# Softmax row sums of a two-layer graph attention: from matmuls against ones to transfers over the partitions

## The chip, the cores and the metric

The kernel runs on one core of one Trainium2 chip. The metric is the device time of one launch in microseconds. Engines are named as in the profile: PE is TensorE (PEld its weight loads), DVE is VectorE, ACT is ScalarE, POOL is GpSimd, SP is SyncE. SP and POOL also issue the transfers (DMA); POOL issues those that add to what stands at the destination.

## What is computed

32 graphs of 512 nodes with 256 features each go through two layers of masked attention with 8 heads of 32 features. Layer 0 masks with the symmetrised adjacency and the diagonal, and has a feed-forward block behind it; layer 1 masks with the adjacency alone. Each layer ends in a residual and a layer norm. All arithmetic is in 32-bit floats.

```python
x = _layernorm(x + L0(x, adj))
x = _layernorm(x + L1(x, adj))
# L0: q, k, v = x @ Wqkv.T + bqkv, heads of 32
#     attn = softmax(where(allowed, q @ k.T / sqrt(32), -inf)); ctx = attn @ v
#     x = LN(x + ctx @ Wo.T + bo); x = LN(x + relu(x @ W1.T + b1) @ W2.T + b2)
# L1: the same attention with mask adj != 0, out = ctx @ Wo.T + bo
```

The part that matters here is the softmax's denominator, the row sum of `exp(scores)` over the 512 keys, for each of 512 queries, 8 heads, 2 layers and 32 graphs.

## The kernel before

Attention is computed transposed. For a group `hg` of four heads (`HPC` = 4) and a block `kc` of 128 keys (`NQ` = 4), one *beat* `k = hg * 4 + kc` makes a tile `p[k]` of 128 keys by 4 heads by 512 queries: `scores` (L345, then the exponential on ACT, L349), `masked` (L354, DVE multiplies by the mask), `product` (L362, TensorE adds values times `p` into PSUM; at the last block ACT copies the result to `cT`, L372). So a layer has 8 beats, and the row sums run over the partitions (keys)[...].

The row sums are made in two steps. First, the four tiles of a group are added into one: `pair` (L377) is a transfer that POOL issues and that adds `p[k + 1]` onto `p[k]`, 1 MB; `fold` (L381) is an addition on DVE. `pair(0)`, `pair(2)` and `fold(2, 2, 0)` leave the sum of group 0 in `p[2]`; `fold(3, 6, 7)`, `pair(4)` and `fold(3, 3, 4)` leave that of group 1 in `p[3]`. Then `sums` (L402) multiplies the tile by a matrix of ones on TensorE, head `j` into the 32 rows from `32 * j` of a PSUM tile, so that every one of these rows holds the sums of that head.

`divide(hg)` (L414 to L421) then runs on DVE: a transpose in blocks of 32 turns the sums of 512 queries into 16 columns, a reciprocal is taken of these, a second transpose spreads it over the rows, and `cT` is multiplied by it. POOL adds the sums and reciprocals to `total` (L417, L418), a running check at the end of the program that tells whether a slower general version is needed. `project` (L461) multiplies `cT` by the output weights; `out0` and `out1` (L449 and the statistics L430, L431) add the residual and start the layer norm. `root` (L436, L437) is the layer norm's inverse square root, on POOL; `norm1` to `norm4` and `offset` (L527) use it. `mlp` (L502) is the second half of the feed-forward block, `out2` its residual.

For the very last attention (`final()`: graph 31, layer 1) `pair` and `fold` do nothing, and `sums` goes over all four tiles with matmuls.

The order is written out by hand: every engine works through its instructions in program order, and each waits for the semaphores of what it needs. `period(a, b, c, d, e)` is one such list, with five graphs in it at different stages: `a` is finishing layer 1, `b` does the feed-forward of layer 0 and starts layer 1, `c` starts layer 0, `d` is loaded and sorted (`load`, `flip`, `sort`, `join`, `entries`, `masks`), `e` is cast. It is called 29 times; `opening` and `closing` hold the first two and last two graphs. SP has its own queue of loads in the same program order and works as far ahead as buffers allow. The tiles `p` have 8 buffers, the PSUM tiles of tag `d`, which the sums share with most other matmuls, have 3.

Of the kernel before, what the change touches and what calls it, by code (L numbers as in the profile page):

```python
# [9 lines left out]
F32 = mybir.dt.float32  # L10
# [4 lines left out]
ALU = mybir.AluOpType  # L15
AX = mybir.AxisListType
# [11 lines left out]
def kernel(ctx: ExitStack, tc: tile.TileContext, t: dict, out: bass.AP):  # L28
# [36 lines left out]
    total = const.tile([P, N // HD], F32, name="total")  # L65
# [84 lines left out]
    def plain(pools: ExitStack):  # L150
        work = pools.enter_context(tc.tile_pool(name="work", bufs=2))
        small = pools.enter_context(tc.tile_pool(name="small", bufs=4))
# [24 lines left out]
        class Graph:  # L177
# [159 lines left out]

            def scores(self, layer, k):
                if k == 0:
                    self.layer, self.p, self.acc = layer, {}, {}  # L340
                hg, kc = divmod(k, NQ)
                s = ps_s.tile([P, HPC, N], F32, tag="s", name=f"psS_{self.b}_{k}")
                for j in range(HPC):
                    at = slice(j * HD, (j + 1) * HD)
                    nc.tensor.matmul(  # L345
                        s[:, j, :], self.kT[at, hg, kc * P : (kc + 1) * P], self.qT[at, hg, :], start=True, stop=True
                    )
                p = work.tile([P, HPC, N], F32, tag="p", name=f"p_{self.b}_{k}", bufs=8)
                nc.scalar.activation(p, s, AF.Exp, scale=SCALE)  # L349
                self.p[k] = p  # L350
# [32 lines left out]
            def add(self, dst, a):  # L383

                if not self.final():
                    nc.gpsimd.dma_start(out=self.p[dst], in_=self.p[a], accum_op=ALU.add)

            def final(self):

                return self.b == B - 1 and self.layer == 1  # L390

            def sums(self, k, hg, first=False, last=False):

                if first:
# [14 lines left out]

            def divide(self, hg):  # L410


                sT = small.tile([P, N // HD, HD], F32, tag="sT", name=f"sT_{self.b}_{hg}", bufs=1)
                nc.vector.transpose(sT.rearrange("p a b -> p (a b)"), self.total[hg])  # L414
                r = small.tile([P, N // HD], F32, tag="r", name=f"r_{self.b}_{hg}")
                nc.vector.reciprocal(r, sT[:, :, 0])
                nc.gpsimd.tensor_tensor(total, total, sT[:, :, 0], ALU.add)  # L417
                nc.gpsimd.tensor_tensor(total, total, r, ALU.add)  # L418
                rT = small.tile([P, N], F32, tag="sT", name=f"rT_{self.b}_{hg}", bufs=1)
                nc.vector.transpose(rT, r[:, :, None].to_broadcast([P, N // HD, HD]))  # L420
                nc.vector.tensor_tensor(self.cT[:, hg, :], self.cT[:, hg, :], rT, ALU.mult)  # L421
# [120 lines left out]
        def period(a, b, c, d, e):  # L542
# [33 lines left out]
            b.root(3, 3, 4)  # L576
# [125 lines left out]
            b.pair(4)  # L702
            c.norm3(1)
            c.norm3(0)
            b.divide(0)


        def opening(a, b, c, d):
# [60 lines left out]
            b.query_key(0, 0, 0)  # L769
            b.cast()  # L770
            a.fold(2, 2, 0)
            a.fold(3, 6, 7)

            b.scores(0, 0)
            a.fold(3, 3, 4)
            a.sums(2, 0, first=True, last=True)
            a.product(6)
            b.scores(0, 1)
            a.residual()
            a.product(7)  # L780
            a.sums(3, 1, first=True, last=True)
            a.divide(0)
            a.divide(1)
            b.scores(0, 2)
            b.query_key(0, 1, 1)
            a.project(0, 0)
            a.out0(0)
            a.out0(1)
# [89 lines left out]
            a.transpose(a.x2, 1)  # L878
            b.fold(3, 6, 7)
            b.fold(2, 2, 0)  # L880
            c.join(0, 0)
            a.query_key(1, 0, 0, 0)
            a.query_key(1, 0, 0, 1)
# [5 lines left out]
            a.query_key(1, 1, 1)  # L889
            a.scores(1, 1)  # L890
            b.fold(3, 3, 4)
            c.join(0, 1)
# [3 lines left out]
            b.divide(0)  # L896
            b.divide(1)
            a.product(0)
            a.scores(1, 2)
            c.value(0, 1)  # L900
# [3 lines left out]
            a.masked(1, 1)  # L904
            a.masked(1, 2)
            a.masked(1, 3)
            b.project(0, 0)
            c.query_key(0, 0, 1)
            b.project(0, 1)
# [24 lines left out]
            b.norm1(3)  # L934
            a.masked(1, 5)
            a.fold(2, 2, 0)
            a.masked(1, 4)
            b.hidden(0, 6)
            b.hidden(0, 4)
# [15 lines left out]
            b.norm2(0)  # L955
            b.norm2(1)
            b.root(3, 0, 2)
            a.divide(0)
            a.pair(4)
            b.norm3(1)  # L960
            b.norm3(0)
# [1 line left out]
        def closing(a, b, c):  # L963
# [12 lines left out]
            a.fold(3, 6, 7)  # L976
            c.masked(0, 0)
            a.fold(3, 3, 4)
            a.sums(3, 1, first=True, last=True)
            c.product(0)  # L980
            c.masked(0, 1)
# [5 lines left out]
            c.once1()  # L987
            c.masked(0, 3)
            c.pair(0)
            a.divide(1)  # L990
# [6 lines left out]
            a.project(1, 0)  # L997
            c.scores(0, 6)
            c.product(2)
            b.root(2, 2, 3)  # L1000
            c.pair(2)
            a.project(1, 1)
            a.out1(0)
# [17 lines left out]
            b.query_key(1, 0, 0, 1)  # L1021
            c.masked(0, 7)
            c.fold(2, 2, 0)
            c.masked(0, 6)
            a.offset(0, 2)
            c.fold(3, 6, 7)
            c.fold(3, 3, 4)
            b.query_key(1, 1, 1)

            b.scores(1, 0)  # L1030
# [9 lines left out]
            b.scores(1, 5)  # L1040
            a.norm4(0)
            c.sums(3, 1, first=True, last=True)
            c.divide(0)
            a.offset(2, 4)
            c.divide(1)
            b.value(1, 0)
            a.norm4(2)
            a.norm4(3)
            b.scores(1, 4)
            c.project(0, 0)  # L1050
            c.out0(0)
            b.query_key(1, 1, 0, 1)
# [68 lines left out]
            b.masked(1, 7)  # L1121
            b.pair(4)
            b.fold(2, 2, 0)
            b.fold(3, 6, 7)
            c.query_key(1, 1, 0, 0)
            c.query_key(1, 0, 0, 1)
# [6 lines left out]
            c.scores(1, 3)  # L1133
            c.value(1, 0)
            b.fold(3, 3, 4)
            b.divide(0)
            b.sums(3, 1, first=True, last=True)
            c.scores(1, 2)
            c.query_key(1, 1, 1)
            b.divide(1)  # L1140
            b.residual2()
            c.residual2()
            c.masked(1, 3)
# [3 lines left out]
            c.masked(1, 1)  # L1147
            c.value(1, 1)
            c.scores(1, 5)
            b.project(1, 0)  # L1150
            c.masked(1, 0)
            c.masked(1, 5)
# [264 lines left out]
```

## Time and profile before

| | us |
|---|---|
| median of 3 runs (lowest, highest) | 3075.76 (3073.19, 3076.84) |
| span of the profiled execution | 3072.4 |
| PE busy | 3049.0 (99%) |
| DVE busy | 2648.1 (86%) |
| ACT busy | 1707.3 (56%) |
| POOL busy | 1039.0 (34%) |
| row-sum matmuls (L402), busy, 1072 records | 139.8 |
| additions by transfer (L377), 189 of 1 MB | 7.7 each, issue to landing |
| time from one period's start to the next | 95.8 |

The page gives the span from the first to the last instruction; the profiled execution's own time is not given beside it, so the runs' median, 3.4 us above the span, stands for what lies around it. A matmul of 32-bit floats leaves two records. Busy time is the time in which an engine has an instruction running; four matmuls on separate quarters of the array overlap, so the mean of one record (598 ns for L402) is longer than the time by which it moves the next one on. DMA has a mean busy share of about 0.7 of the 16 engines in the middle of the run.

### The profile page before, as it was taken

Reading aid. Unit: us, or ns where it says so; the run is one execution under the profiler, and the core shown is the slowest. Engines: PE = TensorE matmul, PEld = TensorE weight load, DVE = VectorE, ACT = ScalarE, POOL = GpSimd, SP = SyncE. Lnnn points to the kernel's source line nnn. Section 1 sums busy time; section 2 is a strip of 40 time slices with the busy share of each in tenths; the row PEclk is TensorE's granted clock in tenths of the full one; section 3 lists DMA queues with packets and bytes.
Section 4 is the critical chain, followed back from the end, with each engine's and each line's share of the span. In section 5 each row is a group of like instructions: output and inputs, shape, how many; then the busy total and the mean of one; then the engine's idle time right before and its main releaser. Section 6 shows DMA issues by size and latency. Waiting matters only on the chain. (4 is left out here: it accounts for less than half of the span.)

```text
span 3072.4 us, 44237 instructions
## 1 busy us (share of the span) xinstructions
PE 3049.0 (99%) x17218; PEld 1728.9 (56%) x17218; DVE 2648.1 (86%) x3458; ACT 1707.3 (56%) x1983; POOL 1039.0 (34%) x1254
## 2 busy tenths in 40 slices
PE   8999999999999999999999999999999999999998
PEld 4555655556555555555555555655556555555564
DVE  6798889888889888898888988889888889888887
ACT  5455565555556555565556655565555556555554
POOL 1333333433334332343323333333433334332332
PEclk9999999999999999999999999999999999999999
DMA  9876677666767666676666766667766767666543
GB/s 207 155 141 129 116 141 145 140 123 126 136 138 148 121 131 124 138 154 122 133 124 136 148 134 131 114 141 145 139 124 126 136 137 148 120 131 124 117 83 70
DMA packets 341064, 406.54 MB, mean 132 GB/s; under 512 B 149616, under 2 KB 315632, under 8 KB 316144
## 3 DMA queue, kind: packets, MB, share of 16 engines
q0 software_dynamic: 95824, 282.09, 51.2%
q1 hardware_dynamic: 245024, 121.56, 16.1%
q8 instruction: 137, 2.24, 0.3%
q14 instruction: 79, 0.65, 0.1%
HBM read 89.01 MB, written 33.55 MB: 40 GB/s over the span
## 5 line engine op out<-in xcount | busy, mean ns | idle before, releaser
L349 ACT ACTIVATE p<-psS 128x2048 f32<-128x2048 f32 x512 | 962.2, 1879 | 657.1 <-PE psS L345 655.4
L354 DVE TENSOR_TENSOR p<-p,m 128x2048 f32<-128x2048 f32 x512 | 1155.4, 2279 | 8.4 <-ACT p L349 8.2
L436 POOL TENSOR_SCALAR rs<-mv 128x2 f32<-128x2 f32 (+1 forms) x320 | 326.3, 1020 | 940.6 <-DVE mv L431 939.7
L345 PE MATMUL psS<-qT,kT 32*128 32x512 f32 x4096 | 583.9, 640 | 2.8 <-ACT p L349 1.3
L362 PE MATMUL psA<-p,v 128*32 128x512 f32 x4096 | 492.7, 598 | 0.9 <-ACT cT L372 0.7
L502 PE MATMUL psF<-w_L_gnn_W,hT 128*128 128x256 f32 x2048 | 468.5, 382 | 0.0
L481 PE MATMUL psH<-xT,w_L_gnn_W 128*128 128x256 f32 x2048 | 467.3, 384 | 0.7 <-DMA w_L_gnn_W<-in_L_gnn_W_dram 0.7
L502 PEld LDWEIGHTS psF<-w_L_gnn_W,hT 128*128 128x128 f32 x2048 | 383.8, 190 | 123.0 <-issue 76.4
L481 PEld LDWEIGHTS psH<-xT,w_L_gnn_W 128*128 128x128 f32 x2048 | 381.4, 190 | 120.3 <-issue 47.9
L381 DVE TENSOR_TENSOR p<-p,p 128x2048 f32<-128x2048 f32 x189 | 429.5, 2286 | 6.4 <-DMA p<-p 4.7
L345 PEld LDWEIGHTS psS<-qT,kT 32*128 32x128 f32 x4096 | 159.9, 182 | 300.5 <-issue 117.2
L437 POOL TENSOR_TENSOR rs<-rs,neg_half 128x2 f32<-128x2 f32 (+1 forms) x320 | 299.6, 936 | 26.8
L362 PEld LDWEIGHTS psA<-p,v 128*32 128x32 f32 x4096 | 109.9, 109 | 315.3 <-issue 234.5
L489 ACT ACTIVATE hT<-psH,c_L_gnn_b 128x256 f32<-128x256 f32 x512 | 215.2, 472 | 120.6 <-PE psH L481 117.3
L417 POOL TENSOR_TENSOR total<-total,sT 128x16 f32<-128x16 f32 x128 | 28.4, 222 | 732.0 <-DVE sT L414 732.0
L461 PE MATMUL psO<-w_L_gnn_Wo,cT 128*128 128x256 f32 x1024 | 241.0, 383 | 0.9 <-DVE cT L421 0.9
L332 PE MATMUL psQK_None<-xT,w_L_gnn_Wqkv 128*128 128x512 f32 x512 | 238.4, 598 | 2.4 <-DMA w_L_gnn_Wqkv<-in_L_gnn_Wqkv_dram 2.4
L372 ACT COPY cT<-psA 128x512 f32<-128x512 f32 x128 | 75.0, 586 | 280.7 <-PE psA L362 280.7
L377 POOL DMA_DIRECT2D p<-p x189 | 188.2, 996 | 117.8 <-PE psA L362 108.7
L449 DVE TENSOR_TENSOR y<-psF,x 128x256 f32<-128x256 f32 x128 | 53.9, 421 | 200.1 <-PE psF L502 197.6
L461 PEld LDWEIGHTS psO<-w_L_gnn_Wo,cT 128*128 128x128 f32 x1024 | 189.3, 190 | 52.0 <-DVE cT L421 23.0
L430 DVE BATCH_NORM_STATS2 st<-y 128x6 f32<-128x256 f32 x384 | 164.3, 428 | 13.1
(68 smaller groups left out, 2930.8 us busy)
## 6 DMA issues: line engine op xcount, KB each, us to landing
p<-p POOLq DMA_DIRECT2D x189, 1024.0 KB, 7.7
x<-in_x_dram SPq DMA_DIRECT2D x64, 512.0 KB, 5.1
x<-bov POOLq DMA_DIRECT2D x64, 512.0 KB, 9.2
code<-in_adj_dram POOLq DMA_DIRECT2D x32, 512.0 KB, 6.6
m<-code SPq DMA_DIRECT2D x32, 512.0 KB, 5.6
x<-s_L_gnn_ln_b POOLq DMA_DIRECT2D x32, 512.0 KB, 10.4
x<-s_L_gnn_b POOLq DMA_DIRECT2D x32, 512.0 KB, 5.4
out_dram<-x SPq DMA_DIRECT2D x32, 512.0 KB, 9.1
```

Source lines behind the costliest of these rows:

```text
L332: nc.tensor.matmul(ps, w[:, i, c * P : (c + 1) * P], self.xT[:, i, at], start=(i == 0), stop=(i == ND - 1))
L345: nc.tensor.matmul(s[:, j, :], self.kT[at, hg, kc * P : (kc + 1) * P], self.qT[at, hg, :], start=True, stop=True)
L349: nc.scalar.activation(p, s, AF.Exp, scale=SCALE)
L354: nc.vector.tensor_tensor(p, p, m[:, k % NQ, None, :].to_broadcast([P, HPC, N]), ALU.mult)
L362: nc.tensor.matmul(self.acc[hg][j * HD : (j + 1) * HD, :], self.v[:, kc, h * HD : (h + 1) * HD], self.p[k][:, j, :], start=(kc == 0), stop ...
L381: nc.vector.tensor_tensor(self.p[dst], self.p[a], self.p[b], ALU.add)
L436: nc.gpsimd.tensor_scalar(rs, self.mv[n][:, a:b, 1:2], EPS, None, ALU.add)
L437: nc.gpsimd.tensor_tensor(rs, rs, neg_half[:, a:b, None], ALU.pow)
L461: nc.tensor.matmul(ps[:, j, :], self.cT[:, k, at], wo[layer][:, k, :], start=(k == 0), stop=(k == ND - 1))
L481: nc.tensor.matmul(ps[:, j, :], w1[:, c, at], self.xT[:, c, h * 2 * P : (h + 1) * 2 * P], start=(c == 0), stop=(c == ND - 1),)
L489: nc.scalar.activation(self.hT[h][:, f + j, :], ps[:, j, :], AF.Relu, bias=b1[:, f + j : f + j + 1])
L502: nc.tensor.matmul(ps, self.hT[h][:, f, j * P : (j + 1) * P], w2[:, f, :], start=(f == 0), stop=(f == NF - 1))
```

## The change

The matmuls against ones go, except for the final attention. In their place `tree(k, hg)` adds over the partitions by transfers: rows 64 to 127 of the tile onto rows 0 to 63 (512 KB), then rows 32 to 63 onto rows 0 to 31 (256 KB), both issued by POOL and adding at the destination. Then SP issues four plain transfers, one for each head, which put the 32 remaining rows of head `j` into rows `32 * j` to `32 * j + 31` of a tile `part` (64 KB each). `part` has one buffer. `divide` transposes `part` instead of the PSUM tile and adds the last 32 rows with a reduction on DVE before the reciprocal. The order changes with it: each `tree` stands behind the `fold` that finishes its tile, and the two `divide` calls of a layer stand next to each other just ahead of its `project`.

The diff, with the hunks of the class and of `period`; those of `opening` and `closing` insert `tree` and move `divide` in the same way.

```diff
@@ -337,7 +337,7 @@
 
             def scores(self, layer, k):
                 if k == 0:
-                    self.layer, self.p, self.acc = layer, {}, {}
+                    self.layer, self.p, self.acc, self.parts = layer, {}, {}, {}
                 hg, kc = divmod(k, NQ)
                 s = ps_s.tile([P, HPC, N], F32, tag="s", name=f"psS_{self.b}_{k}")
                 for j in range(HPC):
@@ -385,18 +385,30 @@
                 if not self.final():
                     nc.gpsimd.dma_start(out=self.p[dst], in_=self.p[a], accum_op=ALU.add)
 
+            def tree(self, k, hg):
+
+                if self.final():
+                    return
+                p = self.p[k]
+                for rows in (P // 2, P // 4):
+                    nc.gpsimd.dma_start(out=p[:rows], in_=p[rows : 2 * rows], accum_op=ALU.add)
+                self.part = small.tile([P, N], F32, tag="part", name=f"part_{self.b}_{hg}", bufs=1)
+                for j in range(HPC):
+                    nc.sync.dma_start(out=self.part[j * HD : (j + 1) * HD, :], in_=p[:HD, j, :])
+                self.parts[hg] = self.part
+
             def final(self):
 
                 return self.b == B - 1 and self.layer == 1
 
             def sums(self, k, hg, first=False, last=False):
 
+                if not self.final():
+                    return
                 if first:
                     self.total[hg] = ps_d.tile([P, N], F32, tag="d", name=f"psR_{self.b}_{hg}")
-                beats = [k]
-                if self.final():
-                    beats = range(hg * NQ, (hg + 1) * NQ) if last else []
-                    first = True
+                beats = range(hg * NQ, (hg + 1) * NQ) if last else []
+                first = True
                 for i in beats:
                     for j in range(HPC):
                         nc.tensor.matmul(
@@ -411,10 +423,16 @@
 
 
                 sT = small.tile([P, N // HD, HD], F32, tag="sT", name=f"sT_{self.b}_{hg}", bufs=1)
-                nc.vector.transpose(sT.rearrange("p a b -> p (a b)"), self.total[hg])
+                sums = small.tile([P, N // HD], F32, tag="sums", name=f"sums_{self.b}_{hg}", bufs=2)
+                if self.final():
+                    nc.vector.transpose(sT.rearrange("p a b -> p (a b)"), self.total[hg])
+                    nc.vector.tensor_copy(sums, sT[:, :, 0])
+                else:
+                    nc.vector.transpose(sT.rearrange("p a b -> p (a b)"), self.parts[hg])
+                    nc.vector.tensor_reduce(sums, sT, AX.X, ALU.add)
                 r = small.tile([P, N // HD], F32, tag="r", name=f"r_{self.b}_{hg}")
-                nc.vector.reciprocal(r, sT[:, :, 0])
-                nc.gpsimd.tensor_tensor(total, total, sT[:, :, 0], ALU.add)
+                nc.vector.reciprocal(r, sums)
+                nc.gpsimd.tensor_tensor(total, total, sums, ALU.add)
                 nc.gpsimd.tensor_tensor(total, total, r, ALU.add)
                 rT = small.tile([P, N], F32, tag="sT", name=f"rT_{self.b}_{hg}", bufs=1)
                 nc.vector.transpose(rT, r[:, :, None].to_broadcast([P, N // HD, HD]))
@@ -553,6 +571,7 @@
             b.hidden(1, 6)
             c.masked(0, 1)
             a.fold(3, 3, 4)
+            a.tree(3, 1)
             c.once()
             c.scores(0, 2)
             c.masked(0, 2)
@@ -564,13 +583,14 @@
             c.product(0)
             b.mlp(2)
             c.residual()
-            a.divide(1)
             b.root(2, 3, 4)
-            a.project(1, 0)
             c.scores(0, 4)
             b.transpose(b.x2, 0)
             b.norm2(3)
             c.masked(0, 3)
+            a.divide(0)
+            a.divide(1)
+            a.project(1, 0)
             c.pair(0)
             b.out2(2)
             b.root(3, 3, 4)
@@ -603,6 +623,7 @@
             b.query_key(1, 0, 0, 0)
             c.masked(0, 6)
             c.fold(2, 2, 0)
+            c.tree(2, 0)
             b.query_key(1, 1, 0, 1)
             a.norm4(0)
             a.norm4(1)
@@ -621,7 +642,7 @@
             b.query_key(1, 0, 1)
             d.entries()
             c.fold(3, 3, 4)
-            c.divide(0)
+            c.tree(3, 1)
             d.load()
             d.flip(0, 0)
             d.sort(0, 0)
@@ -630,7 +651,6 @@
             c.sums(3, 1, first=True, last=True)
             b.masked(1, 2)
             b.scores(1, 1)
-            c.divide(1)
             e.cast()
             b.residual2()
             b.value(1, 0)
@@ -641,6 +661,8 @@
             c.once1()
             b.masked(1, 1)
             b.scores(1, 5)
+            c.divide(0)
+            c.divide(1)
             c.project(0, 0)
             c.project(0, 1)
             b.scores(1, 3)
@@ -688,6 +710,7 @@
             c.mlp(1)
             b.product(3)
             b.fold(2, 2, 0)
+            b.tree(2, 0)
             b.masked(1, 4)
             c.out2(0)
             c.out2(1)
@@ -702,7 +725,6 @@
             b.pair(4)
             c.norm3(1)
             c.norm3(0)
-            b.divide(0)
 
 
         def opening(a, b, c, d):
...
```

More of the change, by code (lines that the diff above doesn't have):

```diff
@@ L771, in opening @@
             a.fold(2, 2, 0)
+            a.tree(2, 0)
             a.fold(3, 6, 7)
@@ L775, in opening @@
             a.fold(3, 3, 4)
+            a.tree(3, 1)
             a.sums(2, 0, first=True, last=True)
@@ L781, in opening @@
             a.sums(3, 1, first=True, last=True)
+            b.scores(0, 2)
+            b.query_key(0, 1, 1)
             a.divide(0)
             a.divide(1)
-            b.scores(0, 2)
-            b.query_key(0, 1, 1)
             a.project(0, 0)
@@ L880, in opening @@
             b.fold(2, 2, 0)
+            b.tree(2, 0)
             c.join(0, 0)
@@ L891, in opening @@
             b.fold(3, 3, 4)
+            b.tree(3, 1)
             c.join(0, 1)
@@ L895, in opening @@
             b.sums(3, 1, first=True, last=True)
-            b.divide(0)
-            b.divide(1)
             a.product(0)
@@ L906, in opening @@
             a.masked(1, 3)
+            b.divide(0)
+            b.divide(1)
             b.project(0, 0)
@@ L936, in opening @@
             a.fold(2, 2, 0)
+            a.tree(2, 0)
             a.masked(1, 4)
@@ L957, in opening @@
             b.root(3, 0, 2)
-            a.divide(0)
             a.pair(4)
@@ L978, in closing @@
             a.fold(3, 3, 4)
+            a.tree(3, 1)
             a.sums(3, 1, first=True, last=True)
@@ L989, in closing @@
             c.pair(0)
-            a.divide(1)
             c.masked(0, 4)
@@ L996, in closing @@
             b.root(2, 3, 4)
-            a.project(1, 0)
             c.scores(0, 6)
@@ L1000, in closing @@
             b.root(2, 2, 3)
+            a.divide(0)
+            a.divide(1)
+            a.project(1, 0)
             c.pair(2)
@@ L1023, in closing @@
             c.fold(2, 2, 0)
+            c.tree(2, 0)
             c.masked(0, 6)
@@ L1027, in closing @@
             c.fold(3, 3, 4)
+            c.tree(3, 1)
             b.query_key(1, 1, 1)
@@ L1042, in closing @@
             c.sums(3, 1, first=True, last=True)
-            c.divide(0)
             a.offset(2, 4)
-            c.divide(1)
             b.value(1, 0)
@@ L1049, in closing @@
             b.scores(1, 4)
+            c.divide(0)
+            c.divide(1)
             c.project(0, 0)
@@ L1123, in closing @@
             b.fold(2, 2, 0)
+            b.tree(2, 0)
             b.fold(3, 6, 7)
@@ L1135, in closing @@
             b.fold(3, 3, 4)
-            b.divide(0)
+            b.tree(3, 1)
             b.sums(3, 1, first=True, last=True)
@@ L1139, in closing @@
             c.query_key(1, 1, 1)
-            b.divide(1)
             b.residual2()
@@ L1149, in closing @@
             c.scores(1, 5)
+            b.divide(0)
+            b.divide(1)
             b.project(1, 0)
```

## The prediction

> **What bounds the kernel now.** I read the page first, then the busy time by stretch, then the timelines of one period in the middle, then the list of waits.
>
> ```profile
> PE 3049.0 (99%) x17218; PEld 1728.9 (56%) x17218; DVE 2648.1 (86%) x3458; ACT 1707.3 (56%) x1983; POOL 1039.0 (34%) x1254
> ```
>
> TensorE has no idle time: 100.00 of 100 us in nearly every stretch of the middle. One period of the hand-written order lasts 95.8 us (the same addition to `total` stands at 1701.04 and at 1796.84 on POOL), and there are 29 periods. That TensorE is full doesn't yet mean that less TensorE work shortens the period, so I look for the second limit.
>
> ```profile
> 1736.92 0.69 DVE L421 TENSOR_TENSOR cT<-cT,rT 128x512 f32<-128x512 f32 x1
> ...
> 1774.55 0.42 DVE L449 TENSOR_TENSOR y<-psF,x 128x256 f32<-128x256 f32 x1 [4.06 <-PE psF L502]
> ```
>
> ```profile
> 1737.33 3.72 PE L461 MATMUL psO<-w_L_gnn_Wo,cT 128*128 128x256 f32 x16
> ...
> 1770.90 3.62 PE L502 MATMUL psF<-w_L_gnn_W,hT 128*128 128x256 f32 x16
> 1774.44 1.06 PE L362 MATMUL psA<-p,v 128*32 128x512 f32 x8
> ```
>
> The first fence is VectorE's timeline, the second TensorE's (start, duration, operation, idle time before it and what ended it). The division of the second head group (L421) ends at 1736.92 + 0.69 = 1737.6, and the projection that needs it (L461) is what TensorE works on from 1737.33, its first half of the contraction needing the other group only. TensorE's second `mlp` (L502) ends at 1774.5, and VectorE, which waited 4.06 us for it, starts `out2(1)` at 1774.55. So there is a ring: TensorE from the projection to `mlp(1)`, 37.1 us; VectorE from `out2(1)` to the next division, 1737.6 + 95.8 - 1774.55 = 58.85 us, nearly without a gap. 37.1 + 58.85 is the period again. **Both the full TensorE and this ring bind.** The list of waits says so too:
>
> ```profile
> DVE y L449 <- PE psF L502: 197.6, 62, 4.9
> PEld psO L461 <- DVE cT L421: 23.0, 30, 1.0
> ```
>
> VectorE waits at one point of each period (two waits, 6.4 us), and the projection's weights wait for the division about once in each: 30 times.
>
> [...]
>
> **The change, part by part.**
>
> *TensorE.* 126 row sums go (64 layer passes of two groups, less the last pass). One moves the next matmul on by 0.88 to 1.00 us (L402 at 1697.29, its successor at 1698.17; the others in the same way), 0.93 on average: 3.7 us a period, 117 us in all. A PSUM buffer is freed too; nothing in the waits asks for one, so I give it nothing.
>
> *VectorE.* `divide` gets a reduction of 128x512. Nearest rows (busy us, mean ns, idle before):
>
> ```profile
> L354 DVE TENSOR_TENSOR p<-p,m 128x2048 f32<-128x2048 f32 x512 | 1155.4, 2279 | 8.4 <-ACT p L349 8.2
> ...
> L421 DVE TENSOR_TENSOR cT<-cT,rT 128x512 f32<-128x512 f32 x128 | 88.6, 692 | 8.7
> ```
>
> [...] I take 0.69, four a period: **2.8 us**, all in the ring. The division now takes 2.46 (1730.40 to 1732.86) + 0.69 = 3.15 us.
>
> *Order.* `c.divide` moves behind `masked(1,0)` and `masked(1,1)`, 2.2 us each from start to start. Two multiplications that came after the projection's release now come before it: **4.4 us** in the ring. The other moved divisions (`b.divide(0)` at the end of the period, `a.divide(1)`) stay inside VectorE's part of the ring and cost nothing themselves.
>
> *POOL and SP.* Four trees a period, each two accumulating transfers (512 and 256 KB) and four plain ones of 64 KB. I need times for them:
>
> ```profile
> p<-p POOLq DMA_DIRECT2D x189, 1024.0 KB, 7.7
> ...
> x<-s_L_gnn_b POOLq DMA_DIRECT2D x32, 512.0 KB, 5.4
> ...
> kT<-v SPq DMA_DIRECT2D x248, 64.0 KB, 3.9
> ```
>
> A lone 1 MB addition keeps the engines at share 1.0 with about 200 GB/s, so 5.2 of its shortest 7.0 us are data and 1.8 fixed. [...]That makes the halves 1.8 + 2.6 = 4.4 and 1.8 + 1.3 = 3.1 us[...]. I take 5.0 and 3.5. Four plain copies: three issues of 0.6 and a landing of 2.1 to 3.9, I take 4.2 us together. All four trees add about 5.1 us each of full DMA load, 20 us on top of 0.69 x 95.8 = 66: it fits, so load is not the matter; latency is.
>
> What stands behind the waits: POOL's small operations for the layer norms, which VectorE needs at once. After a transfer the first of them is slow:
>
> ```profile
> 1702.38 0.94 POOL L377 DMA_DIRECT2D p<-p  x1
> 1704.56 2.16 POOL L436 TENSOR_SCALAR rs<-mv 128x1 f32<-128x1 f32 x1 [1.25 <-DVE mv L431]
> 1706.80 0.58 POOL L437 TENSOR_TENSOR rs<-rs,neg_half 128x1 f32<-128x1 f32 x1
> ```
>
> Both `part` tiles of a pass share one buffer: the second group's four copies wait until `divide(0)` has read the first, and SP holds the next graph's loads behind them. Those loads ran far ahead so far (x at 1709.95, its two flips from 1710.44 to 1726.7, wanted by `join` at 1743.96). Now they start at about t = 81 of the walk below; a flip (5.8), four sorting copies (2.5) and their landing (3.9) end at 94, and `join` is wanted 6.6 us after the projection's start, at 92.6: hidden but for about 1 us, which I leave to the high end. POOL has eight issues more a period, some 6 us on an engine that is a third busy: nothing, apart from the roots. `p[2]` and `p[3]` stay taken until their copies are read; by the order of the changed kernel their buffers go to `scores(0,6)`, `scores(1,6)` and `scores(1,4)`, over 8 us later: nothing, or 2 us if a copy is that late.
>
> *The walk.* t = 0 is `mlp(1)`'s end. VectorE, by the starts of the timeline:
> - `out2(1)`, `norm2`, `norm3` to 6.9; without `b.divide(0)` the additions and two multiplications end at 15.9 with `fold(3,3,4)`. Tree: first transfer 16.0 to 21.0, second issued 21.1, then two bias additions (issues until 24.4), then `root(2,3,4)`: 2.2 + 0.6 from 24.1, done 27.0. VectorE wants it in `norm2(3)` at 19.6: **stall 7.5**.
> - `masked(0,3)` to 30.4; `divide(0)`; its transpose ends at 31.2, the second copies land at 35.4: `divide(1)` **stalls 1.9**, ends 38.5. `norm3(3)` waits for a root behind `pair(0)`: **stall 1.6**.
> - The same work as before then brings `fold(2,2,0)` to its end at 58.5. Tree: 58.6 to 63.8 (behind `pair(4)`), then `root(4,2,4)` done at 67.4; `offset` wants it at 60.7: **stall 6.8**. (Before, this place had 0.97 for a transfer, which goes.)
> - `fold(3,3,4)` to 69.8, three multiplications to 76.4, `divide(0)` to 79.5. Tree 69.9, 75.0, 78.5; copies land 82.8: `divide(1)` **stalls 3.3**, ends 86.0.
>
> Against 58.85 this is +27.2: 4.4 + 2.8 + 21.1 - 1. TensorE's 37.1 us after it has no sum in it and stays, so **the period is 123 us**; the 3.7 us saved become idle time. Over 29 periods 789 us; the ten groups in opening and closing at the same 6.8 us each, 68. The profiled execution spans 3072.4, the page gives nothing around it, and the median is 3.4 above. 3072 + 857 + 3 = 3932. Some divisions at the ends stand farther from their trees; I take **3900**.
>
> **Rivals.**
> - *The transfers hide, TensorE sets the end*: 3076 - 117 = 2959. For it: TensorE is full, and 3.7 us a period really go. Against: the ring has no slack for 7.2 us of VectorE work, whatever the transfers do. It decides if the ring has at least that much. Chance 0.02.
> - *The transfers hide, the ring grows by VectorE's work alone*: 7.2 x 31.5 = 227, 3300. It needs POOL to pass the waits; its order puts the roots behind the second transfer. Chance 0.08.
> - *DMA load becomes the bound*[...]. Chance 0.03.
> - *The transfers aren't waited for, or the edit does less than it says*: 3076. Chance 0.01.
>
> The walk: 0.86.
>
> **How the numbers follow.** Low end of the walk: 4.4 and 3.1 us, roots fast (0.3), stalls about 13, +19 a period, 3670; if half of those hide, 3500. [...] Range 3500 to 4200; it leaves out the first, second, third and fourth rivals and a twentieth of the walk. A measurement of this kernel tells about 0.2% from no change. Faster 0.02, same 0.01, slower 0.97.
>
> **What would show it.** TensorE's busy time falls by about 117 to 131 us (L402's row) while its idle time rises to some 900 us, most of it put to `psO <- DVE cT`. Waits of VectorE: `z` for `rs` near 7 us, once a period; `ms` for `rs` near 7; `sT` for the part transfers 2 to 3, twice; POOL stands about 5 us at each second transfer. Wrong if POOL issues the second transfer at once, if the roots come on time, if VectorE still waits for `psF` only as now and the period is under 103 us, or if TensorE stays full.

## The result, and the profile after

The kernel after takes 4350.68 us (median of four runs, 4334.83 to 4357.13); the kernel before took 3075.05 beside it. The ratio is 1.4142, interval 1.4125 to 1.4159. The forecast was 3900 with a range of 3500 to 4200, whose upper end rested on estimates of the author that no trace of before showed: the direction came true, the size did not.

The profiled execution spans 4355.2 us. First the page: busy time by engine, and the granted TensorE clock in 40 slices.

```profile
PE 3156.8 (72%) x16210; PEld 1806.2 (41%) x16210; DVE 2764.8 (63%) x3586; ACT 1693.5 (39%) x1983; POOL 1081.0 (25%) x1506
...
PEclk8978888888888888888988888888898888988888
```

TensorE, full before, is now busy 72% of the span. Its busy microseconds rose although the row-sum matmuls (139.8 us) are gone: the mean granted clock is 0.854 instead of 0.999, and the same matmuls last longer (the output projections 430.4 us in all, 241.0 before). Read alone, that busy time hides what happened; the waits of the kernel after tell it (total us, number, longest).

```profile
PE psO L479 <- DVE cT L439: 1143.0, 127, 19.0
...
POOL p L394 <- DMA p<-p: 638.9, 123, 9.4
...
DVE sT L431 <- DMA part<-p: 525.0, 72, 17.0
...
DVE z L463 <- POOL rs L455: 211.0, 62, 8.2
...
DVE ms L545 <- POOL rs L455: 177.5, 32, 13.0
```

TensorE stands at the output projection for the division, 1143 us in all. VectorE stands at three places: for the sums' copies, and for two roots on POOL. POOL stands 638.9 / 123 = 5.2 us at each second addition, for the first to land; no trace of before showed this wait. All of these kinds of wait were forecast. Their sizes are the matter.

The mean period comes from the starts of `masks` (L222) through the middle of each trace: before (2699.1 - 612.1) / 22 = 94.9 us, after (2630.1 - 727.6) / 14 = 135.9 us, so +41.0 where the forecast had +27.2 (its 95.8 us for a period of before was a single one). Here is where VectorE stands in the second half of one period after (start, duration, operation, idle time ahead of it and what ended it).

```profile
2177.03 0.16 DVE L545 SCALAR_TENSOR_TENSOR ms<-mv,rs 128x2 f32<-128x2 f32 x1 [5.40 <-POOL rs L455]
2186.43 0.71 DVE L431 STREAM_TRANSPOSE sT<-part 128x512 f32<-128x512 f32 x1 [0.42 <-DMA part<-p]
...
2205.47 0.71 DVE L431 STREAM_TRANSPOSE sT<-part 128x512 f32<-128x512 f32 x1 [15.84 <-DMA part<-p]
```

The last line is `divide(1)` of layer 0, the end of the walk. It waits 15.84 us, where the walk had 3.3. The queues of SP and of POOL at that time say what it waits for:

```profile
2183.13 1.27 SPq L213 DMA_DIRECT2D m<-code  x1
2184.45 12.47 SPq L218 DMA_TRANSPOSE m<-code  x4
2197.47 2.42 SPq L397 DMA_DIRECT2D part<-p  x4
```

```profile
2185.87 0.78 POOL L394 DMA_DIRECT2D p<-p  x1 [5.26 <-DMA p<-p]
2186.38 0.80 POOL L204 DMA_DIRECT2D code<-in_adj_dram  x1
2186.90 1.64 POOL L169 DMA_DIRECT2D x<-bov  x1
```

SP issues the second set of copies at 2197.47, just when it is through with four transposes of the next graph's code table (12.47 us). The second addition, issued at 2185.87 beside them, lands after 11.5 us, at about 2197.4; the same transfer at another place (2175.12) takes 4.5. So SP's queue and the late addition both hold the copies back, until about the same moment, and these lines don't tell which of them counts. And POOL puts two more 512 KB transfers, `code` and `bov`, right behind it.

### The profile page after: what moved, and what is told of

The parts are those of the page before. It is cut to its first block, busy times and chain, and to the rows that moved or that the text cites. A ratio compares the mean times of both kernels' runs of the same rounds, so it can differ in the third digit from the quotient of the medians.

```text
span 4355.2 us, 44207 instructions
## 1 busy us (share of the span) xinstructions
PE 3156.8 (72%) x16210; PEld 1806.2 (41%) x16210; DVE 2764.8 (63%) x3586; ACT 1693.5 (39%) x1983; POOL 1081.0 (25%) x1506
## 4 chain that ended last, share of the span: by engine, by line
PE 32%; DMA 24%; issue 14%; DVE 12%; SPq 9%; POOL 6%; ACT 3%; POOLq 0%; DVEq 0%; ACTq 0%
DMA p<-p 12%; PE psO L479 6%; PE psF L520 5%; PE psQK_None L332 5%; PE psS L345 5%; DMA v<-in_x_dram 4%; PE psH L499 4%; SPq L397 4%; PE psA L362 4%; DMA part<-p 4%; DVE p L354 3%; ACT p L349 2%; DMA kT<-v 2%; SPq L218 2%; POOL x L169 2%
## 5 line engine op out<-in xcount | busy, mean ns | idle before, releaser
L479 PE MATMUL psO<-w_L_gnn_Wo,cT 128*128 128x256 f32 x1024 | 430.4, 591 | 1143.0 <-DVE cT L439 1143.0
L479 PEld LDWEIGHTS psO<-w_L_gnn_Wo,cT 128*128 128x128 f32 x1024 | 295.5, 304 | 1285.4 <-DVE cT L439 1216.8
L394 POOL DMA_DIRECT2D p<-p x252 | 206.5, 824 | 1297.4 <-DMA p<-p 638.9
L431 DVE STREAM_TRANSPOSE sT<-part 128x512 f32<-128x512 f32 x126 | 89.4, 709 | 526.1 <-DMA part<-p 525.0
L454 POOL TENSOR_SCALAR rs<-mv 128x2 f32<-128x2 f32 (+1 forms) x320 | 249.0, 778 | 680.0 <-DVE mv L449 678.5
L435 POOL TENSOR_TENSOR total<-total,sums 128x16 f32<-128x16 f32 x128 | 62.4, 488 | 802.6 <-DVE sums L432 779.3
L455 POOL TENSOR_TENSOR rs<-rs,neg_half 128x2 f32<-128x2 f32 (+1 forms) x320 | 243.5, 761 | 26.7
L377 POOL DMA_DIRECT2D p<-p x189 | 189.6, 1003 | 191.7 <-PE psA L362 146.3
```

The lines of the kernel that those rows point to most:

```text
L454: nc.gpsimd.tensor_scalar(rs, self.mv[n][:, a:b, 1:2], EPS, None, ALU.add)
L455: nc.gpsimd.tensor_tensor(rs, rs, neg_half[:, a:b, None], ALU.pow)
L479: nc.tensor.matmul(ps[:, j, :], self.cT[:, k, at], wo[layer][:, k, :], start=(k == 0), stop=(k == ND - 1))
```

## The experiments

Runs are compared by their medians; each ratio is to the kernel before on the same chip. Periods are means worked out as above.

### Cutting the transfers away

x1 leaves out all transfers of the trees, x2 the copies alone, x3 the additions alone.

```diff
-  for rows in (P // 2, P // 4):                                   # x1, x3
-      nc.gpsimd.dma_start(out=p[:rows], in_=p[rows : 2 * rows], accum_op=ALU.add)
-  self.part = small.tile(...); 4 x nc.sync.dma_start(...)         # x1, x2
+  self.parts[hg] = p[:, 0, :]                                    # x1, x2
```

> The changed kernel with all transfers of the trees left out (the sums are not formed: divide transposes and reduces one head of the folded tile where it lies, and the reciprocal is taken of ones). VectorE's work, the order and TensorE's work are those of the changed kernel. Ring theory: VectorE's chain is 7.2 us longer than before with nothing waited for, minus about 1, so a period of 102 to 103 us and 3270 to 3330 us in all, part of it a slower clock after TensorE's new gaps. Rival, TensorE alone sets the end: period 92 us, 2960 us. Rival, the moved order costs more than VectorE's work because other waits open: above 3400 us.

Measured: 3433.27 us, ratio 1.1168 (1.1146 to 1.1190), period 106.2. With no transfer to wait for, the kernel is still 359 us slower than before beside it (3074.11). So it isn't TensorE's own work that sets the end. Its mean granted clock is 0.950, that of before 0.999. The time lies above the ring's forecast, where the rival of the moved order had put it. (Beside the lines shown, x1 to x3 and x8 take the reciprocal of ones.)

> The changed kernel without the four plain copies of each tree (divide transposes one head of the tile after the two additions, so the sums are wrong in three heads; the reciprocal is taken of ones). POOL's stalls stay: z for rs near 6, ms for rs near 5.4 us a period. If SP's copies and what stands around them in its queue make the long wait of the second division, both waits of sT (2.65 and 15.84 us a period) nearly vanish: at most 2 us stay, -16 to -18 us a period, 3800 to 3880 us. Rival, the additions themselves land late: the waits stay at 5 us or more, above 3950 us.

Measured: 4000.66 us, ratio 1.3014 (1.2965 to 1.3062), period 124.6: over 100 us slower than expected. The waits of `sT` nearly went, as the theory said (74.8 us over the run, 525.0 after), but that of `ms` for its root rose to 290.6 us over 31 (177.5 over 32 after): part of the gain was handed on.

> The changed kernel without the two additions of each tree (the copies move rows 0 to 31 of the folded tile, so three quarters of the keys are missing from the sums; the reciprocal is taken of ones). POOL's stalls go: z and ms wait for rs under 2 us together, -10 us a period. The copies can start right behind the fold, so the second division of layer 0 waits 2 to 5 us instead of 15.84, if the latency of the tree and SP's queue add up as I think: period 110 to 114 us, 3550 to 3680 us. Rival, SP's queue alone makes the long wait (the transposes ahead of the copies take 12 us whatever the additions do): it stays near 10 us, 3750 to 3850 us.

Measured: 3616.61 us, ratio 1.1764 (1.1741 to 1.1788), period 112.1, as expected. The additions alone cost 4001 - 3433 = 567 us, the copies alone 183, both together 4351 - 3433 = 917: 167 us more than the two apart. One place where they meet is the code table: its transposes land in 4.6 us (median) with the additions alone, in 4.5 with the copies alone and in 11.1 with both. That this is the whole of the 167 us is not shown.

### The place of the divisions, without transfers

x8 is x1 with the divisions of `period` and `a.project(1, 0)` put back where before had them.

```diff
-            a.divide(0)
-            a.divide(1)
-            a.project(1, 0)
+            a.divide(1)          # behind c.residual()
+            a.project(1, 0)      # behind b.root(2, 3, 4)
-            c.divide(0)
-            c.divide(1)
+            c.divide(0)          # behind c.fold(3, 3, 4)
+            c.divide(1)          # behind b.scores(1, 1)
+            b.divide(0)          # behind c.norm3(0)
```

> The kernel of x1_no_transfers (the trees' transfers left out, so the divisors are wrong and a constant is taken in their place), with the divisions of the repeated period and a.project(1, 0) back at the places of the kernel before. x1_no_transfers took 3433 us, 357 above before. Theory 'the place is most of it': with the 4.4 us of the two masked and the 2.3 us of half clock at the projections gone, 6.7 us a period, 3200 to 3270; what is then left above 3075 is the four reductions (2.8 us a period, 80 us) and little else. Rival 'the place is worth its VectorE work alone': 4.4 us a period, about 3305. Rival 'the matmul sums that are gone from TensorE leave gaps and a lower clock wherever the divisions stand': within 60 us of 3433.

Measured: 3164.82 us, ratio 1.0299 (1.0279 to 1.0319), period 97.1. The new place costs 3433 - 3165 = 268 us, 9.1 us a period; the two `masked` put ahead of the divisions explain 4.4 of it. From the start of `out2(1)` to the end of `divide(1)` of layer 0, VectorE takes 59.9 us in x8 (1532.11 to 1592.00) and 68.3 in x1 (1553.68 to 1622.01), 8.4 more: the two `masked`, and waits that x8 doesn't have there. VectorE's timeline of x1:

```profile
1565.89 2.29 DVE L354 TENSOR_TENSOR p<-p,m 128x2048 f32<-128x2048 f32 x1 [0.82 <-ACT p L349]
...
1575.22 0.48 DVE L458 SCALAR_TENSOR_TENSOR z<-cent,rs,x 128x256 f32<-128x256 f32 x1 [0.78 <-POOL rs L450]
...
1586.60 0.41 DVE L531 TENSOR_SCALAR x<-z,mv,rs 128x256 f32<-128x256 f32 x1 [0.88 <-POOL rs L450]
1587.72 0.42 DVE L462 TENSOR_TENSOR y<-psO,x 128x256 f32<-128x256 f32 x1 [0.71 <-PE psO L474]
```

They stand ahead of the moved divisions of layer 1 and behind them: for exponents, for two roots and for the projection of layer 1 (1.35 us in most other periods). With a second wait of 0.23 us for exponents they make 3.4 us. Why each of them is late wasn't followed up.

At layer 0 TensorE's clock has a small part in it. Here are TensorE's timelines of the projection of layer 0, first x1, then x8 in two periods in a row:

```profile
1618.97 1.22 PE L474 MATMUL psO<-w_L_gnn_Wo,cT 128*128 128x256 f32 x2 [3.85 <-DVE cT L434]
1622.07 4.88 PE L474 MATMUL psO<-w_L_gnn_Wo,cT 128*128 128x256 f32 x14 [1.88 <-DVE cT L434]
```

```profile
1494.59 4.98 PE L474 MATMUL psO<-w_L_gnn_Wo,cT 128*128 128x256 f32 x14 [2.08 <-DVE cT L434]
...
1592.05 3.29 PE L474 MATMUL psO<-w_L_gnn_Wo,cT 128*128 128x256 f32 x14 [2.09 <-DVE cT L434]
```

In x1 TensorE runs dry for 3.85 and 1.88 us, and the projection then takes 4.88 us. In x8 it takes 4.98 us in 14 of the 29 periods and 3.29 in the other 15. From the slow one to the next projection pass 97.46 us, from the fast one 96.81, so the slow clock at this place costs 0.65 us a period. `out0(0)` waits 3.02 us for the projection in x1 and not at all in this stretch of x8, where the two `masked` stand between; but from the end of `divide(1)` to the next `out2(1)` x1 takes 37.5 us (1622.01 to 1659.49) and x8 36.9 behind the fast projection (1592.00 to 1628.93), so that wait adds little. The granted clock in the stretch of the long wait of the kernel after (2185 to 2205) is 0.50, and x8 shows 0.50 (1496 to 1498) behind a wait of only 2.08 us too.

What x8 still has above before, 2.2 us a period, answers to four reductions of 0.686 us (2.7), less a little.

### The queue ahead of the copies

x4, complete, has only `d.entries()` (the code table and its transposes) moved ahead, behind `a.project(1, 1)`.

```diff
             a.project(1, 1)
+            d.entries()
...
-            d.entries()          # ahead of c.fold(3, 3, 4)
```

> The changed kernel complete, with d.entries() of period (one load and four transposes of the adjacency, 1.3 + 12.5 us of issue on SP) moved ahead to just behind a.project(1, 1), so that they don't stand between the two groups of part copies of layer 0. If SP's queue is what my walk missed, the wait of the second division falls from 15.8 to 5 to 7 us a period: 4350 - 29 x 10 = 4060 us (ratio to before about 1.32). Rival, the copies land late because the 16 engines are loaded (the cast and the bias additions that POOL issues behind the tree): the wait stays above 11 us, over 4200 us.

Measured: 4261.17 us, ratio 1.3867 (1.3842 to 1.3891), period 132.6. VectorE's timeline of x4, the same place:

```profile
2158.30 0.71 DVE L431 STREAM_TRANSPOSE sT<-part 128x512 f32<-128x512 f32 x1 [10.45 <-DMA part<-p]
```

The time missed the expected 4060 and is above the rival's 4200; the wait lies between the two. Moving the code table was worth 5.4 of the 15.84 us, half of what the first theory wanted; the second addition lands in 4.7 again, so the 5.4 hold both the shorter queue and the faster addition, and x4 doesn't separate them. The four copies still take 6.8 us each with `code` (11.1) and `bov` (14.9) under way. x5 therefore moves these two as well.

```diff
-            e.cast()             # ahead of b.value(1, 0)
-            b.residual2()
...
             c.project(0, 1)
+            e.cast()
+            b.residual2()
```

> The kernel after, complete, with the earlier place of d.entries() from the last experiment, and e.cast() and b.residual2() (two transfers of graph inputs that POOL issues right behind the second addition of the tree of layer 0, group 1) moved behind c.project(0, 1). Theory 'the small transfers share the DMA engines with the copies of the sums': the wait of divide(1) of layer 0 on its part falls from 10.45 us to about 5 to 6, some 5 us a period, so 4090 to 4150 us. Rival 'the 10.45 us are the chain of the tree's own two additions and four copies': the wait stays at 9 to 11 us and the time within 15 us of 4261.

Measured: 4278.49 us, ratio 1.3933 (1.3901 to 1.3964), period 133.7. The time missed its expectation; the wait did what the theory said. POOL's issue of the first addition of that tree in x5, then VectorE's timeline, and ACT's at the place between:

```profile
2009.49 0.90 POOL L394 DMA_DIRECT2D p<-p  x1 [2.70 <-DVE p L381]
```

```profile
2024.32 0.71 DVE L431 STREAM_TRANSPOSE sT<-part 128x512 f32<-128x512 f32 x1 [5.24 <-DMA part<-p]
...
2053.73 2.29 DVE L354 TENSOR_TENSOR p<-p,m 128x2048 f32<-128x2048 f32 x1 [4.76 <-ACT p L349]
```

```profile
2051.33 0.59 ACT L322 COPY v<-psV 128x512 f32<-128x512 f32 x1 [10.16 <-DMA kT<-v]
```

`divide(1)` now waits 5.24 us instead of 10.45; from the first issue of the tree to the division pass 14.8 us, where the walk had 12.9. But the moved transfers run beside the sorting of the next graph; ACT waits 10.16 us (5.06 in x4) for that landing, TensorE for ACT, and VectorE for late exponents. Over the run, the waits of `sT` fell from 405 to 264 us and those of `masked` rose from 69 to 221. The gain was handed on whole. x6 takes up the other term, the roots.

```diff
             c.fold(2, 2, 0)
+            a.root(4, 2, 4)
             c.tree(2, 0)
...
             c.masked(0, 0)
+            a.fold(3, 3, 4)
+            a.tree(3, 1)
```

> The kernel of x5_small_transfers_late, and a.root(4, 2, 4) moved ahead of c.tree(2, 0) on POOL, and a.fold(3, 3, 4) with a.tree(3, 1) moved one masked ahead, behind c.masked(0, 0), so that POOL is through with the tree sooner when root(2, 3, 4) comes. Theory 'VectorE waits for the roots only because POOL, in order, stands at the second addition of a tree': the wait of ms falls from 5.4 us to under 1, that of z from 6.1 to about 3.3, together some 7 to 8 us a period: about 220 us less than x5, 3870 to 3930 if x5 meets its theory. Rival 'the wait is handed on: what VectorE does sooner finds the sums' transfers not landed': the waits of sT on part grow by what the roots gave, and the time stays within 60 us of x5.

Measured: 4213.62 us, ratio 1.3706 (1.3666 to 1.3746), period 131.0. The wait of `ms` went (173.6 to 13.9 us), that of `z` fell (211.0 to 154.2), 217 us together; the waits of `sT` rose by 93 and those of `fold` for its pair by 63. So 65 us of some 217 came through, close to the rival. Last, x10 puts the two small transfers where the sort has landed.

```diff
-            e.cast()             # x6: behind c.project(0, 1)
-            b.residual2()
...
             c.hidden(0, 6)
+            e.cast()
+            b.residual2()
```

> The kernel of x6_roots_first with e.cast() and b.residual2() moved once more, behind c.hidden(0, 6), so that POOL issues their transfers after the sort of d has landed. In x5 and x6 the wait of divide(1) on its part had fallen to about 5 us, but ACT then waited 10.2 us (5.1 before) for the sort's transfer to cast v, TensorE for ACT, and two masked for their exponents (4.3 and 3.4 us in x6). Theory 'one load of small transfers, and whoever waits for the next landing pays': the two waits of masked go, 7 to 8 us a period, 4210 less about 215, 3980 to 4050. Rival 'the exponents are late for another reason, or the load meets the next landing at the new place': within 60 us of 4214.

Measured: 4018.13 us, ratio 1.3073 (1.3054 to 1.3092), period 124.0: in the expected range. The waits of `masked` for exponents are down from 196.5 to 38.0 us. One wait is new, 84.2 us of VectorE for another bias addition to land (7.2 in x6). From the kernel after to x10 nothing but the order changed, and 333 of 1276 us came back.

### TensorE's clock with the transfers in place

x7 is the kernel after with idle time of TensorE filled by matmuls whose results are overwritten.

```diff
+                if h == 0:
+                    for _ in range((56, 14)[layer]):
+                        nc.tensor.matmul(ps[:, 0, :], wo[layer][:, 0, :P], wo[layer][:, 0, :D], start=True, stop=True)
```

> The kernel after, complete, with matmuls put ahead of both first output projections, whose results are overwritten: 56 of them in layer 0 and 14 in layer 1 (128x128 by 128x256), so that TensorE is busy through most of the 17.8 and 4.6 us in which it waits for cT. Theory 'the granted clock falls to half in these gaps and the work behind them pays': the projections take 3.7 us again instead of 5.09 and 6.26, the mean clock rises from 0.85 to over 0.93, and the time falls by 3.9 us a period or a little more, to 4200 to 4245. Rival 'the slow projections lie beside the other waits': the clock rises, the time stays within 30 us of 4350; it goes above 4350 if the filling runs past the division.

Measured: 4363.32 us, ratio 1.4184 (1.4149 to 1.4220), no better than after. TensorE's and VectorE's timelines of x7 in layer 0, in a period in which the filling is long enough:

```profile
2070.22 3.29 PE L482 MATMUL psO<-w_L_gnn_Wo,cT 128*128 128x256 f32 x14 [1.35 <-DVE cT L439]
```

```profile
2071.82 0.42 DVE L467 TENSOR_TENSOR y<-psO,x 128x256 f32<-128x256 f32 x1 [1.66 <-PE psO L482]
```

The mean granted clock rose from 0.854 to 0.967. Here the projection takes 3.29 us and `out0(0)` waits 1.66; in the kernel after these are 4.67 to 6.32 us and 3.02. But the filling is long enough in only 13 of the 29 periods; in the others but one the projection of layer 0 takes 4.67 to 6.25 us. In layer 1 it was too short throughout: in this period the projection follows a wait of 5.33 us and takes 6.28. Over the run VectorE's waits for the projections fell by no more than 8.5 us (142.0 to 133.5), while those for the copies of the sums rose from 525.0 to 547.0. So the 3.9 us a period of the theory didn't come, as the rival said. What the slow clock costs where it is wholly taken away, this run doesn't settle.

### A version that might beat both

Before has its ring and TensorE both full, so a tree can pay only where its landing has time and the ring is shortened as well. x9 has the order alone: one `query_key` out of TensorE's part of the ring, one `fold` into the 4.07 us in which VectorE waits for `mlp(1)`.

```diff
-            d.query_key(0, 1, 1)
-            c.mlp(1)
             b.product(3)
+            c.mlp(1)
+            d.query_key(0, 1, 1)
...
             c.out2(0)
+            b.fold(3, 6, 7)      # from the next period's start
```

> The kernel before, complete, with its matmul sums, and three moves in the repeated period: b.product(3) ahead of c.mlp(1), d.query_key(0, 1, 1) behind it, and b.fold(3, 6, 7) between c.out2(0) and c.out2(1), where VectorE waits 4.07 us. They shorten the ring of TensorE and VectorE by about 3 us a period and leave TensorE's work as it is. Theory 'TensorE is busy throughout and sets the time of before': 3068 to 3080, no change beyond the measurement. Rival 'the ring sets it': 3 us a period less, about 2990.

Measured: 3082.11 us, ratio 1.0026 (1.0015 to 1.0036), period 95.2: 8 us slower, 2 us above the expected range. TensorE's busy time is 3056.9 us, 99% of the span. A shorter ring brings nothing as long as TensorE is full.

```diff
             b.fold(2, 2, 0)
+            b.tree(2, 0)         # sums(2, 0) of layer 1 left to it
...
-            b.divide(0)          # at the period's end
+            a.divide(0)          # ahead of a.divide(1)
```

> The kernel of x9_order_only, complete, and one of the four trees of the kernel after: b.tree(2, 0) behind b.fold(2, 2, 0) of layer 1 in place of the eight matmuls of sums(2, 0), its division next to divide(1) at the place that divide(1) has in before, so that some 30 us lie between the tree and its use. The other three divisors stay with TensorE. Theory 'a tree pays where its landing has time and no root or small transfer stands behind it': TensorE loses 1.0 us a period, 29 us in all, 3040 to 3052. Rival 'its transfers delay the code transposes and the roots behind them as in after': 3075 or more.

Measured: 3182.37 us, ratio 1.0368 (1.0339 to 1.0398). VectorE's line and SP's queue in one period of x11:

```profile
2137.33 2.29 DVE L382 TENSOR_TENSOR p<-p,p 128x2048 f32<-128x2048 f32 x1 [9.27 <-DMA p<-p]
```

```profile
2117.88 12.55 SPq L218 DMA_TRANSPOSE m<-code  x4
```

The code transposes stand behind the tree's copies on SP and now run beside `pair(4)`, issued at 2119.78: it lands after 17.5 us, and the fold waits for it. In x12 the transposes go first.

```diff
             b.fold(2, 2, 0)
-            b.tree(2, 0)
             b.masked(1, 4)
+            e.entries()
+            b.tree(2, 0)
```

> The kernel of x11_one_tree, complete, with b.masked(1, 4) and the transfers of the next code table (e.entries()) ahead of b.tree(2, 0) on SP. In x11 the four code transposes stood behind the four copies of the tree, were issued 66 us later than in before, and ran beside pair(4), which then landed after 17.5 us (7.5 in before); the second fold waited 9.3 us for it, and TensorE 7.5 us for the fold. Theory 'the loss of x11 is this one collision': pair(4) lands in 7 to 8 us again, the wait of the fold goes, and what TensorE no longer does shows: 3045 to 3065. Rival 'the tree and the transposes now meet each other, the second addition is late, and the roots behind it on POOL with it': above 3075, with waits of z on rs of several us.

Measured: 3115.71 us, ratio 1.0133 (1.0116 to 1.0150), period 96.3. The collision is gone (`pair(4)` lands in 7.7 us, no root is late), but the kernel stays slower than before. TensorE's waits in x12:

```profile
PE psO L485 <- DVE y L473: 21.2, 28, 1.0
PE psT L303 <- DVE x L469: 13.2, 29, 0.6
PE psT L303 <- DVE x L542: 9.9, 29, 2.4
```

So the time is the rival's and its reason is not. TensorE lost 31 us of row-sum matmuls (140.5 us in x9, 109.6 here) and gained 44 us of waits for VectorE, whose list got a reduction and the division of group 0 moved from the end of one period into the next. That these waits come from the moved division is likely, not shown. No version here beats the kernel before.

## Why the prediction was right or wrong

The growth of the period, term by term. The measured terms are differences of periods: x8 - before, x1 - x8, after - x1.

| term | predicted | measured |
|---|---|---|
| reductions (and no sums on TensorE) | 2.8 | 97.1 - 94.9 = 2.2 |
| place of the divisions | 4.4 | 106.2 - 97.1 = 9.1 |
| transfers | 21.1 - 1 = 20.1 | 135.9 - 106.2 = 29.7 |
| together | 27.2 (rounded) | 41.0 |

- **What bounds the kernel**: right. The ring closes over both engines: x8 has no transfers and less TensorE work and is slower; x9 has a shorter ring and is no faster. (That 37.1 + 58.85 give the period proves nothing, since the second number was reckoned from the period; the argument is that neither part has a gap.)
- **The reduction**: right. Its row in the profile after has a mean of 686 ns, where 0.69 us was estimated from an addition of the same shape (692 ns in before):

```profile
L432 DVE TENSOR_REDUCE sums<-sT 128x16 f32<-128x512 f32 x126 | 86.4, 686 | 4.4
```

- **Order**: the step that failed second. The two multiplications (4.4 us) came as reckoned, but the other moved divisions, which "stay inside VectorE's part of the ring and cost nothing themselves", opened waits there: in x1 VectorE's part has 8.4 us more than in x8, 4.4 of them the multiplications and 3.4 waits for exponents, roots and the projection of layer 1. TensorE's slow clock behind its wait at layer 0 cost 0.65 us a period in x8.
- **The walk, layer 1 and the offset**: right in kind, a little too dear. `z` waited 6.06 us (7.5 predicted), `divide(1)` 2.65 (1.9), `ms` 5.40 (6.8). `norm3(3)` didn't wait the 1.6 forecast; `out1(0)` waited 1.48 for the projection there, and that the two are near is luck.
- **The walk's last line**: the step that failed. "`divide(1)` stalls 3.3" was 15.84. The second addition and the copies had been priced without the transfers that run beside them, and SP's queue had been looked at only for what the copies delay, not for what stands ahead of them. By x4 and x5, taken away in this order, the 15.84 us are 5.4 for the code table, 5.2 for `code` and `bov`, and 5.2 for the tree itself, of which the walk had 3.3. All five waits sum to 31.4 us in that period where the walk had 21.1, 10.3 more; the table's transfers are 9.6 more. "Load is not the matter; latency is" was wrong with it: the mean load fits, but the moment of each transfer doesn't.
- **The second rival** (ring growth by VectorE's work alone, 3300) is what x1 measures, at 3433: short by the same order term. The third, load as the bound, was priced by the author's estimate and didn't happen: the queues' packets took 69% of the 16 engines' span after and 68% before.
- **Opening and closing**: 68 us predicted; 1275.6 - 29 x 41.0 leaves 87.
- **The signs**: the waits were named rightly. That TensorE's busy time would fall by 117 to 131 us was wrong: it rose by 108, with the clock at 0.854.

## What to carry to other kernels

When a step gives work to transfers, list for each moment not only what the new transfers delay but what is already queued ahead of them and lands beside them: the same 256 KB took 4.5 us at one place and 11.5 at another. When work only changes its place in a ring, look also at what it had covered there. Moving such a transfer away shows its price only if nobody is waiting where it goes: x5 gave back all that it won, x10 the same move at another place kept it. And a saving on an engine is no credit once something else sets the time; here TensorE came back slower from its gaps as well (in the kernel after the projection takes 5.09 us behind a wait of 17.81 us, with a granted clock of 0.50 from 2205 to 2210; in x7 it takes 3.29 behind 1.35).

## What the runs showed of the hardware that was not expected

- The four code transposes land in 2.7 us (median) in before and in x1, and in 11.1 in the kernel after; moved ahead (x4) they take 4.0. No other kind of transfer stretched so far from before to after. Here are the transfers in the kernel after (KB each, median us from issue to landing):

```profile
p<-p POOLq DMA_DIRECT2D x126, 512.0 KB, 5.6
...
p<-p POOLq DMA_DIRECT2D x126, 256.0 KB, 4.7
part<-p SPq DMA_DIRECT2D x504, 64.0 KB, 3.1
```

- Half the bytes cost little less, by the medians of the kernel after: 1 MB of addition 7.6 us, 512 KB 5.6, 256 KB 4.7. For the two smaller ones the prediction had worked out 4.4 and 3.1 from the 1 MB addition of before (7.0 us at the shortest) and taken 5.0 and 3.5; why they take longer, no run here tells.
- TensorE's clock can differ behind the same gap: in x8 a wait of 2.08 or 2.09 us is followed by a granted clock of 0.50 in one period (1496 to 1498) and 1.00 in the next (1592 to 1598). What decides it, no run here tells.
